# Four graph layers in one kernel: the last rows of the output in long operations, with TensorE adding x and h, and three hand-written orders for layer 3

## The chip, the core and the metric

The kernel runs on one core of a Trainium2 chip. The metric is the device time in microseconds (us) of one execution, given as the median of several runs. The profile is of one execution, and its span (first to last instruction) is a little shorter than the device time.

## What is computed

Four layers work on 3327 nodes with 64 features and one dense 3327 x 3327 matrix `adj`; each adds its result to x. Layers 0 to 2 are a gated graph network of two rounds, a hyperbolic one, and a weighted sum over neighbours. The change lies in layer 3, whose reference is, cut down:

```python
h = jnp.maximum(_layernorm(x, axis=-1), 0.0)
x_tan = _logmap0(h, C)
left, right = x_tan @ att_W[:D] + att_b, x_tan @ att_W[D:]
adj_att = jax.nn.sigmoid(left + right.T) * adj
x_local = _logmap(h[:, None, :], h[None, :, :], C)        # for every pair of nodes
support_t = jnp.einsum('ij,ijd->id', adj_att, x_local)
x = x + _proj(_expmap(h, support_t, C), C)
```

So for every pair of nodes there are a distance function, a sigmoid and a product with `adj`, then sums over the neighbours (a vector of 64 and a few single sums for every node), and at the end a formula for each node that gives two factors, ka and ch, with output = x + ka * (the summed vector) + ch * h.

## The kernel before

Nodes are padded to 26 blocks of 128 and lie in pairs of blocks, 13 columns in two groups: the first (columns 0 to 5) and the second (6 to 12). Layers 0 to 2 stream `adj` from memory and are not touched.

Layer 3 has no scheduler: each engine runs its instructions in the order in which Python emits them. `PHASES` cuts the pairs of columns into 13 phases; the first four need the second group alone. A phase has two halves (b = 0, 1), and its work is cut into steps:

- `distances` (L1199, TensorE) writes scalar products to a PSUM pair, `gelus` (L1209) and `square` (L1219, both ScalarE) make the distance function of them.
- `tanh_d` (L1232) and `tanh_t` (L1255) on ScalarE make the attention for the direct and for the turned (symmetric) pairs; `attention_d`, `attention_t` (L1266, VectorE) multiply it with `adj`, whose tiles come in four slots, in order of use.
- `turned` (L1293, TensorE) transposes the distance function into the other PSUM pair, and `factors_t` (L1303) and `factors_d` (L1284, VectorE) multiply it in.
- `gather_t`, `gather_d` and `singles` (all recorded at L1306, TensorE) add the sums up in PSUM banks.

The order of the steps is written out by hand in `ORDER3`: one list for the start, and one that is run for every phase. In a name such as `gelus.0.1.0` the first number says by how many phases the step is late (0 for the current phase, 1 for the one before, -1 for the next), the others name half and chunk. A `tick` moves the generators of `Weave` on by a step. The one that matters is `nodes3` for the first group: it prepares that group's nodes while phase 0 runs. Its parts are the LayerNorm (L973 to L1002, with the table loads of ScalarE at L992 and L965), xd (L1004), the transposes of xd (L502) and their copies xs (L1024) and xw (L1025, L1026), the attention products (L1033), the packs and rows of bf16 terms (L1073 to L1097, with transposes at L1092), and the attention rows leftb (L1115 to L1120).

The end is `finish_f` for the second group and `finish` for the first: copies of the sums from PSUM (L1376, L1378), their products and squares (L1385, L1387), small sums (L1395), the single sums turned to nodes (copied at L1439, multiplied with `pick` at L1444 into the bank of the small sums, `dots`), and the summed vectors transposed to nodes (L1406), which stay in PSUM as `nat`. About 30 small VectorE operations (L1459 to L1496) make ka and ch. The output then comes block by block: ScalarE multiplies h with ch for 24 blocks (L1504), VectorE does nat * ka + x for each of 26 (L1507), adds the two for three groups of 8 blocks (L1512) and does the last two one by one (L1515), and four stores go out (L1518).

Of the kernel before, what the change touches and what calls it, by code (L numbers as in the profile page):

```python
# [12 lines left out]
AF = mybir.ActivationFunctionType  # L13
# [5 lines left out]
D = 64  # L19
P = 128  # L20
# [63 lines left out]
class Weave:  # L84
# [2 lines left out]
    def __init__(self):  # L87
        self.running = []

    def add(self, gen, after=1, behind=None):  # L90
        self.running.append([gen, after, behind])
        return gen

    def runs(self, *gens):
# [2 lines left out]
    def tick(self):  # L97
        for item in list(self.running):
            if self.runs(item[2]):
                continue  # L100
            item[1] -= 1
            if item[1] <= 0:
                try:
                    item[1] = next(item[0]) or 1
                except StopIteration:
                    self.running.remove(item)

# [82 lines left out]

def order3(text):
    r = []
    for line in text.split("\n"):
        for name, *args in (w.split(".") for w in line.split()):
            r.append((name, *map(int, args)))
    return r
# [4 lines left out]
    order3(t)  # L203
    for t in (
        """
        distances.0.0.0 gelus.0.0.0 distances.0.0.1 tick.0 tanh_t.0.0.0 tanh_t.0.1.0
        attention_t.0.0 tick.0 gelus.0.0.1 distances.0.1.0 square.0.0 tanh_d.0.0 tanh_t.0.0.1
        gelus.0.1.0 attention_d.0.0 tanh_t.0.1.1 distances.0.1.1 tick.1 tick.0 tick.0 gelus.0.1.1
        tick.0 tick.0 square.0.1 turned.0.0.0
        """,  # L210
        """
        factors_t.1.0.0 tick.0 distances.0.0.1 tick.1 turned.1.0.1 tanh_t.0.0.0 attention_d.1.0
        tick.1 singles.2.1 gelus.0.0.1 distances.0.1.0 tick.1 square.0.0 factors_t.1.0.1 tick.0
        turned.1.1.0 gelus.0.1.0 tanh_d.0.0 factors_d.1.0 tick.1 tick.0 tick.0 end.2
        attention_t.1.1 gather_t.1.0.0 tick.0 factors_t.1.1.0 distances.0.1.1 singles.1.0
        gelus.0.1.1 square.0.1 turned.1.1.1 attention_d.1.1 tanh_t.0.0.1 tick.1 distances.-1.0.0
        tanh_t.0.1.0 tick.0 factors_t.1.1.1 tick.0 factors_d.1.1 tanh_d.0.1 tick.0 turned.0.0.0
        attention_t.0.0 tanh_t.0.1.1 gelus.-1.0.0 gather_t.1.0.1 gather_t.1.1.0 gather_d.1.0
        gather_t.1.1.1 gather_d.1.1
        """,  # L220
    )
]


class Stream:
# [67 lines left out]
def gnn_kernel(ctx: ExitStack, tc: tile.TileContext, t, out):  # L293
# [169 lines left out]
    def big(g, name):  # L463

        if g.part is None:
            a = p0.tile([P, GROUPS[1].nb, D], F32, name=name, tag="b_" + name)
        else:

            if name not in bigs:
                bigs[name] = p0.tile([P, GROUPS[1].nb, D], F32, name=name, tag="b_" + name)  # L470
            a = bigs[name][:, 6 * g.part :, :]
        return a[:, : g.nb, :]

    def flat(a):
        return a.rearrange("p a d -> p (a d)")

    def pair(i):

        return ps.tile([P, 1024], F32, name="pair", tag=f"pair{i}")

    def bank(i):
        return ps.tile([P, 512], F32, name="bank", tag=f"bank{i}")
# [678 lines left out]
    def columns(a, n):  # L1161
        return a[:, : 2 * n * P].rearrange("p (k c) -> p k c", k=2)
# [142 lines left out]
    def add(out, lhsT, rhs):  # L1305
        T.matmul(out, lhsT=lhsT, rhs=rhs, start=False, stop=True, skip_group_check=True)  # L1306

    @step3
    def gather_d(m, b):
        a = columns(dirs[m, b], PHASES[m].n)  # L1310
        for c, ts, first in PHASES[m].runs:
            for p, o, lo, hi in runs(ts, place):
                for k in range(2):
                    add(
                        p[k * D : (k + 1) * D, o : o + (hi - lo) * P],
                        xd[:, 2 * c + b, :],
                        a[:, k, (first + lo) * P : (first + hi) * P],
                    )
# [18 lines left out]
    @step3  # L1337
    def singles(m, b):

        nonlocal late_  # L1340
        sums_ = ps_
        if (m, b) == (n_all - 1, 1):

            sums_ = late_ = pair(0)[:, : 2 * P]
            V.memset(late_, 0.0)
        a = columns(dirs[m, b], PHASES[m].n)
        direct, turned_ = [], []
        for c, ts, first in PHASES[m].runs:
            i = 0
            while i < len(ts):  # L1350
                n = min(2 - ts[i] % 2, len(ts) - i)
                o = ts[i] % 2 * P
                for k in range(2):
                    rhs = a[:, k, (first + i) * P : (first + i + n) * P]
                    direct.append(((k, 1 - b, slice(o, o + n * P)), ts[i], 2 * c + b, rhs))
                i += n
        for e, (_, c, j) in enumerate(PHASES[m].turned):
            o = c % 2 * P
            for h_ in range(2):
                rhs = trs[m, b][:, (2 * e + h_) * P : (2 * e + h_ + 1) * P]  # L1360
                turned_.append(((h_, b, slice(o, o + P)), c, 2 * j + b, rhs))
        while direct or turned_:
            for q, most in ((direct, 2), (turned_, 4)):
                for _ in range(min(most, len(q))):
                    single(sums_, *q.pop(0))
# [37 lines left out]
    def by_nodes(g, m, out_, lo, hi):  # L1403

        for c in range(lo, hi):
            T.transpose(  # L1406
                out_[:, (c - lo) * P : (c - lo + 1) * P], m[:, c * P : (c + 1) * P], ident
            )
        for k in range(2 * lo, 2 * hi):
            nat[2 * g.c0 + k] = out_[:, (k - 2 * lo) * D : (k - 2 * lo + 1) * D]  # L1410

    nat, dots = {}, None

    def finish_f():
        nonlocal dots
# [16 lines left out]
    def finish():  # L1432
# [1 line left out]
        parts_ = [(0, 512, x2_), (512, g.w, ps_[:, 2 * P :])]  # L1434
        m = copied(g, parts_)
        ws_ = squares(g, parts_, m)
        pp = flat(big(GROUPS[1], "sq"))[:, : 4 * P].rearrange("p (s i c) -> p s i c", s=2, i=2)
        for s, a in enumerate((ps_, late_)):
            S.activation(pp[:, s], a[:, : 2 * P].rearrange("p (i c) -> p i c", i=2), AF.Copy)  # L1439
        for a, b, _ in parts_:  # L1440
            added(g, ws_, a // P, b // P)
        for i in range(2):
            for s in range(2):
                T.matmul(  # L1444
                    dots[:, 64:96].rearrange("p (r i h) -> p i r h", i=2, h=2)[:, i],
                    lhsT=pp[:, s, i],
                    rhs=pick,
                    start=s == 0,
                    stop=s == 1,
                )  # L1450
        by_nodes(g, m, pair(1), 0, g.n)
        ds, hs, ss = dots[:, 64 : 64 + NB], dots[:, :NB], dots[:, 32 : 32 + NB]


        f = wide3("f", "d2")
# [43 lines left out]
            for b in range(2)  # L1499
        )  # L1500

        steps_ = [(0, 8), (8, 16), (16, 24), (24, NB)]
        for k in range(24):
            S.activation(w2[:, k, :], h[:, k, :], AF.Copy, scale=ch[:, k : k + 1])  # L1504
        for lo, hi in steps_:
            for k in range(lo, hi):
                V.scalar_tensor_tensor(  # L1507
                    w1[:, k, :], nat[k], ka[:, k : k + 1], xn[:, k, :], op0=OP.mult, op1=OP.add
                )
        for lo, hi in steps_:  # L1510
            if hi < NB:
                V.tensor_add(w1[:, lo:hi], w1[:, lo:hi], w2[:, lo:hi])  # L1512
            else:
                for k in range(lo, hi):
                    V.scalar_tensor_tensor(  # L1515
                        w1[:, k, :], h[:, k, :], ch[:, k : k + 1], w1[:, k, :], op0=OP.mult, op1=OP.add
                    )
            nc.sync.dma_start(out[:, lo:hi, :], w1[:, lo:hi])  # L1518

    def bound():  # L1520

# [188 lines left out]


    turn["banks"] = (1,)
    gen_s = weave.add(nodes3(gs_, m_s))

    with ExitStack() as cf:
        wk = cf.enter_context(right("wkf"))

        ps_, x2_, late_ = bank(0), None, None
        V.memset(ps_, 0.0)

        within = n3.tile([1, 1], I32, name="within")
        final = None
        for m, order in [(0, ORDER3[0])] + [(m, ORDER3[1]) for m in range(n_all + 2)]:
            for name, late_by, *args in order:
                if name == "tick":

                    if late_by or m < BETWEEN:  # L1730
                        weave.tick()
                elif have(m - late_by) and (m - late_by, name, *args) not in made3:
                    made3.add((m - late_by, name, *args))
                    for _ in STEPS3[name](m - late_by, *args) or ():
                        pass
            if m == WITHIN + 1:
                ok = nc.values_load(within, min_val=0, max_val=1)
        weave.until(final)
        finish()
# [372 lines left out]
```

## Time and profile before

| | |
|---|---|
| time, median of 3 runs | 701.61 us (699.39 to 702.45) |
| span of the profiled execution | 696.4 us |
| mean granted TensorE clock | 0.966 |
| TensorE (PE) busy | 632.6 us, 91% |
| VectorE (DVE) busy | 460.0 us, 66% |
| ScalarE (ACT) busy | 399.3 us, 57% |
| chain that ended last | PE 73%, DMA 11%, DVE 8%, ACT 5% |
| layer 3, first distances to last instruction | from 423.5 us to 696.4 us |

On a page, the busy tenths show for each of 40 slices how full an engine was, and PEclk the TensorE clock that was granted, in tenths. Where an engine sat idle, the profile names what ended the wait. The chain that ended last is followed back from the last instruction: at each step to what released it. A line of code such as L1306 can be that of a helper that several steps use; then the tiles tell which step it is.

### The profile page before, as it was taken

How to read it: one execution, taken by the hardware profiler on the slowest of the kernel's cores; microseconds unless marked ns; L12 is line 12 of the kernel's file. 1: busy time of each engine (PE TensorE's matmuls, PEld its weight loads, DVE VectorE, ACT ScalarE, POOL GpSimd, SP SyncE). 2: the span in 40 equal slices, each digit the busy share in tenths (PEclk: the TensorE clock that was granted, in tenths of full speed). 3: DMA queues.
4: the chain of work that ended last, by engine and by line, in shares of the span. 5: the costliest groups of instructions: out<-in, count | busy, mean ns of one | idle time of the engine just before them, and what ended most of it. 6: DMA issues, size and time to landing. Idle time of an engine off the chain costs nothing.

```text
span 696.4 us, 13369 instructions
## 1 busy us (share of the span) xinstructions
PE 632.6 (91%) x5648; PEld 358.8 (52%) x5648; DVE 460.0 (66%) x745; ACT 399.3 (57%) x575; POOL 5.9 (1%) x11
## 2 busy tenths in 40 slices
PE   3988999999979999879998996599999999999990
PEld 2433343344324333457875663466666666666770
DVE  4323766444678605786457656489889998888776
ACT  3102200311464203588888788599999898898814
POOL 0000000000000000200000000000000000000000
PEclk9999999999999999999999999599999999999995
DMA  8999998399967999988787863036676666656401
GB/s 342 416 418 416 382 361 299 134 388 416 417 263 279 412 421 416 410 303 292 284 317 261 303 203 135 0 118 201 201 223 210 209 200 201 198 185 198 150 3 53
DMA packets 32611, 185.18 MB, mean 266 GB/s; under 512 B 3616, under 2 KB 4384, under 8 KB 32544
## 3 DMA queue, kind: packets, MB, share of 16 engines
q1 hardware_dynamic: 32544, 184.25, 71.8%
q8 instruction: 46, 0.75, 0.4%
q14 instruction: 21, 0.17, 0.1%
HBM read 183.39 MB, written 0.85 MB: 265 GB/s over the span
## 4 chain that ended last, share of the span: by engine, by line
PE 73%; DMA 11%; DVE 8%; ACT 5%; issue 1%; SPq 0%; ACTq 0%; DVEq 0%
PE bank L627 24%; PE bank L1306 17%; DMA adj<-in_adj 10%; PE pair L1199 8%; PE pair L1293 6%; PE pair L1605 6%; PE bank L1629 5%; PE pair L731 2%; ACT w L1617 1%; DVE mask L1574 1%; PE pair L532 1%; PE bank L1395 1%; DVE w L1507 1%; DMA xn<-in_x 1%; PE bank L1033 1%
## 5 line engine op out<-in xcount | busy, mean ns | idle before, releaser
L627 PE MATMUL bank<-adj,m_a 128*64 128x384 f32 (+1 forms) x832 | 157.3, 524 | 7.5 <-DMA adj<-in_adj 6.7
L627 PEld LDWEIGHTS bank<-adj,m_a 128*64 128x64 f32 x832 | 57.6, 139 | 97.0 <-issue 73.8
L1617 ACT ACTIVATE w<-pair,ebias 128x896 uint16<-128x896 f32 (+1 forms) x101 | 93.8, 953 | 17.0 <-PE pair L1605 15.7
L627 PE MATMUL bank<-adj,m_b 128*64 128x384 f32 (+1 forms) x416 | 76.7, 515 | 0.8 <-ACT hm L716 0.8
L1574 DVE TENSOR_SCALAR mask<-adj 128x1792 bf16<-128x1792 f32 (+1 forms) x52 | 53.8, 1054 | 25.9 <-PE pair L1605 24.1
L1255 ACT ACTIVATE tr<-leftb,righth 128x256 f32<-128x256 f32 x156 | 66.4, 495 | 0.0
L1303 DVE SCALAR_TENSOR_TENSOR tr<-pair,tr 128x1024 f32<-128x1024 f32 (+3 forms) x52 | 50.0, 961 | 23.1 <-PE pair L1293 20.8
L359 DVE SCALAR_TENSOR_TENSOR edges<-adj,edges 128x1792 bf16<-128x1792 f32 (+1 forms) x24 | 44.9, 1890 | 28.6 <-DMA adj<-in_adj 28.5
L1209 ACT ACTIVATE sq<-pair 128x1024 f32<-128x1024 f32 (+1 forms) x52 | 47.4, 912 | 23.9 <-PE pair L1199 22.7
L1629 PE MATMUL bank<-w,m_b 128*64 128x384 bf16 (+1 forms) x416 | 60.6, 341 | 0.0
L1199 PE MATMUL pair<-xs 64*128 64x512 f32 (+3 forms) x120 | 55.6, 549 | 1.2 <-ACT sq L1209 1.2
L1199 PE MATMUL pair<-xs,xw 64*128 64x512 f32 (+3 forms) x120 | 55.6, 549 | 1.1 <-ACT sq L1209 1.1
L716 ACT ACTIVATE hm<-bank 64x384 f32<-64x384 f32 (+1 forms) x8 | 4.1, 512 | 88.2 <-DVE mh L715 88.0
L1293 PE MATMUL pair<-ident,sq 128*128 128x128 f32 x312 | 46.6, 286 | 6.6 <-ACT sq L1219 6.3
L1284 DVE SCALAR_TENSOR_TENSOR dir<-sq,dir 128x1792 f32<-128x1792 f32 (+2 forms) x27 | 52.4, 1945 | 0.0
L1266 DVE SCALAR_TENSOR_TENSOR dir<-dir,adj 128x1792 f32<-128x1792 f32 x26 | 52.4, 2015 | 0.0
L627 PEld LDWEIGHTS bank<-adj,m_b 128*64 128x64 f32 x416 | 29.0, 137 | 44.9 <-issue 42.4
L1293 PEld LDWEIGHTS pair<-ident,sq 128*128 128x128 f32 x312 | 34.1, 143 | 28.9 <-issue 11.9
L1232 ACT ACTIVATE dir<-leftb,righth 128x1792 f32<-128x1792 f32 (+6 forms) x38 | 48.5, 1307 | 0.0
L1219 ACT ACTIVATE sq<-sq,hg 128x1792 f32<-128x1792 f32 x26 | 46.5, 1790 | 0.7
L1266 DVE SCALAR_TENSOR_TENSOR tr<-tr,adj 128x1280 f32<-128x1280 f32 (+2 forms) x26 | 45.5, 1750 | 0.0
L1306 PE MATMUL bank<-dir,xd 128*64 128x384 f32 (+3 forms) x264 | 43.6, 460 | 0.0
(305 smaller groups left out, 983.5 us busy)
## 6 DMA issues: line engine op xcount, KB each, us to landing
adj<-in_adj SPq DMA_DIRECT2D x110, 896.0 KB, 5.8
adj<-in_adj SPq DMA_DIRECT2D x93, 768.0 KB, 8.2
adj<-in_adj SPq DMA_DIRECT2D x12, 640.0 KB, 4.0
out<-w SPq DMA_DIRECT2D x3, 256.0 KB, 3.2
xn<-in_x SPq DMA_DIRECT2D x3, 192.0 KB, 4.8
w_l<-in_w_l SPq DMA_DIRECT2D x1, 460.0 KB, 9.8
xn<-in_x SPq DMA_DIRECT2D x1, 256.0 KB, 6.7
w_all<-in_w_all SPq DMA_DIRECT2D x1, 67.5 KB, 12.7
```

The lines of the kernel that those rows point to most:

```text
L627: T.matmul(acc[q][h * D : (h + 1) * D, : hi - lo], lhsT=m[:, k, :], rhs=a[:, h * g.w + lo : h * g.w + hi], start=first, stop=last,)
L1199: T.matmul(p[:, o : o + n], lhsT=l, rhs=r, start=not rows, stop=rows)
L1232: S.activation(columns(dirs[m, b], ph.n)[:, :, first * P : first * P + n], left_of(ph.g)[:, :, o : o + n], AF.Tanh, bias=righth[:, 2 * c + ...
L1255: S.activation(a[:, e * 2 * P : (e + 1) * 2 * P].rearrange("p (b c) -> p b c", b=2), left_of(ph.s)[:, :, o : o + P], AF.Tanh, bias=righth[ ...
L1266: V.scalar_tensor_tensor(a[:, :w], a[:, :w], 1.0, stream.tile(stream.now), op0=OP.add, op1=OP.mult)
L1284: V.scalar_tensor_tensor(a[:, :, cs], s[:, :, cs], HD, a[:, :, cs], op0=OP.add, op1=OP.mult)
L1293: T.transpose(p[:, o : o + P], columns(sqs[m, b], PHASES[m].n)[:, k, i * P : (i + 1) * P], ident,)
L1303: V.scalar_tensor_tensor(a, pts.pop((m, k, "t"))[:, :n], HD, a, op0=OP.add, op1=OP.mult)
L1306: T.matmul(out, lhsT=lhsT, rhs=rhs, start=False, stop=True, skip_group_check=True)
L1574: V.tensor_scalar(masks[n][:, :w], a, 0.0, None, op0=OP.not_equal)
L1617: S.activation(w, e, AF.Relu, bias=ebias)
L1629: T.matmul(acc2[i][q][h * D : (h + 1) * D, : hi - lo], lhsT=p[:, 2 * c + a, :], rhs=ws[n][:, h * g.w + lo : h * g.w + hi].bitcast(BF16), s ...
```

## The change

It has four parts.

1. Output rows in long operations. For the blocks 12 to 25, TensorE writes x to two PSUM banks (an fp32 product with the identity) and adds ScalarE's products of h and ch. VectorE multiplies nat with ka for many blocks at once, ka being broadcast along the features, and then adds the bank. Blocks 6 to 11 are done by VectorE alone and are stored first; blocks 0 to 5 have x added by VectorE, and h by way of ScalarE. The aim is fewer and longer operations on VectorE, and output that is stored as it becomes ready.
2. The single sums of one half go to the node form earlier, before the last `gather_d`, and both halves have their result in a PSUM bank of their own (`ds_`) instead of in `dots`.
3. `ORDER3` has three lists: one for the start, one for the phases in between, one for the last phase. In the first, `turned.0.0.0` stands behind the first `distances` of the next phase, and `gelus.0.1.1` behind more ticks.
4. `WAITS3` says after how many ticks each step of the first group's `nodes3` is made.

```diff
-    def add(self, gen, after=1, behind=None):
-        self.running.append([gen, after, behind])
+    def add(self, gen, after=1, behind=None, waits=()):
+        self.running.append([gen, after, behind, list(waits)])
...
                     item[1] = next(item[0]) or 1
+                    if item[3]:
+                        item[1] = item[3].pop(0)
...
-        distances.0.0.0 gelus.0.0.0 distances.0.0.1 tick.0 tanh_t.0.0.0 tanh_t.0.1.0
-        attention_t.0.0 tick.0 gelus.0.0.1 distances.0.1.0 square.0.0 tanh_d.0.0 tanh_t.0.0.1
-        gelus.0.1.0 attention_d.0.0 tanh_t.0.1.1 distances.0.1.1 tick.1 tick.0 tick.0 gelus.0.1.1
-        tick.0 tick.0 square.0.1 turned.0.0.0
+        distances.0.0.0 gelus.0.0.0 distances.0.0.1 tanh_t.0.1.0 tick.0 tanh_t.0.1.1 tick.0 tick.0
+        tick.1 gelus.0.0.1 square.0.0 distances.0.1.0 gelus.0.1.0 tick.0 distances.0.1.1 tick.0
+        tick.0 tick.0 gelus.0.1.1 tick.0 tick.0 square.0.1 tick.1 tick.0 tick.1 tick.1 tick.0
+        tick.1 tick.1 distances.-1.0.0 turned.0.0.0 tick.0 tick.0 tanh_d.0.1 tick.0 gelus.-1.0.0
...
     @step3
     def gather_d(m, b):
+        nonlocal pp_
+        if (m, b) == (n_all - 1, 1):
+            assert (m, "singles", 0) in made3
+            pp_ = flat(big(GROUPS[1], "sq"))[:, : 4 * P].rearrange("p (s i c) -> p s i c", s=2, i=2)
+            copied_singles(0, ps_)
...
-            sums_ = late_ = pair(0)[:, : 2 * P]
+            ends_ = pair(0)
+            sums_ = late_ = ends_[:, : 2 * P]
             V.memset(late_, 0.0)
+            ds_ = ends_[:, 512:544]
+            picked(0)
...
-        for k in range(24):
+        for lo, hi, a in sums_x:
+            T.matmul(a, lhsT=ident, rhs=flat(xn[:, lo:hi]), start=True, stop=False)
+        for k in [*range(12, NB), *range(6)]:
             S.activation(w2[:, k, :], h[:, k, :], AF.Copy, scale=ch[:, k : k + 1])
-        for lo, hi in steps_:
-            for k in range(lo, hi):
-                V.scalar_tensor_tensor(
-                    w1[:, k, :], nat[k], ka[:, k : k + 1], xn[:, k, :], op0=OP.mult, op1=OP.add
-                )
...
+        for lo, hi, a in sums_x:
+            T.matmul(a, lhsT=ident, rhs=flat(w2[:, lo:hi]), start=False, stop=True)
...
+        times(6, 12, a[:, 6 * D :])
+        plus(6, 12, xn[:, 6:12])
+        V.tensor_mul(w2[:, 6:12], h[:, 6:12], bc(ch[:, 6:12]))
+        plus(6, 12, w2[:, 6:12])
+        store(6, 12)
+        for lo, hi, b in larger[::-1]:
+            times(lo, hi, b)
+        times(0, 6, a[:, : 6 * D])
+        plus(0, 6, xn[:, 0:6])
+        for lo, hi, b in sums_x:
+            plus(lo, hi, b.rearrange("p (k d) -> p k d", d=D))
+            store(lo, hi)
+        plus(0, 6, w2[:, 0:6])
+        store(0, 6)
...
-    gen_s = weave.add(nodes3(gs_, m_s))
+    gen_s = weave.add(nodes3(gs_, m_s), waits=WAITS3)
...
-        for m, order in [(0, ORDER3[0])] + [(m, ORDER3[1]) for m in range(n_all + 2)]:
+        begin, loop, rest = ORDER3
+        orders = [(0, begin)] + [(m, loop) for m in range(1, n_all - 1)] + [(n_all - 1, rest)]
+        for m, order in orders:
```

The loop list differs from the one before in a few places, among them `tanh_d.0.1`, which stands ahead of `tanh_t.0.1.0`, and `gather_t.1.1.1`, which stands ahead of `gather_t.1.1.0`. The last list takes the steps of the last two phases together and puts `turned.1.1.0` ahead of more ticks, and so ahead of the small sums of `finish_f`.

## The prediction

> **What bounds the kernel now.** I read the page first: the busy slices and the granted TensorE clock of the whole span, to see where TensorE is not the limit.
>
> ```profile
> PE   3988999999979999879998996599999999999990
> ACT  3102200311464203588888788599999898898814
> PEclk9999999999999999999999999599999999999995
> ```
>
> TensorE is near full almost everywhere. Two places matter to this change: a dip two thirds of the way through, and the last slices, empty and at the low clock. Next the busy time by stretches of 10 us, which puts times to them (columns: busy us of PE, PEld, DVE, ACT, POOL, each with a count; then granted clock, DMA share, GB/s).
>
> ```profile
> 430.00:440.00 10.00, 2.60 (x15) 1.41 (x12) 7.52 (x19) 8.63 (x12) 0.00 (x0) 0.73 0.00 1
> 440.00:450.00 10.00, 6.67 (x27) 4.93 (x27) 2.42 (x10) 3.80 (x6) 0.00 (x0) 0.50 0.00 0
> 450.00:460.00 10.00, 9.71 (x82) 6.34 (x80) 8.27 (x26) 7.94 (x10) 0.00 (x0) 0.75 0.02 4
> 600.00:610.00 10.00, 10.00 (x120) 6.50 (x113) 9.51 (x6) 9.97 (x17) 0.00 (x0) 1.00 0.68 225
> 660.00:670.00 10.00, 10.00 (x148) 7.47 (x146) 9.90 (x8) 0.84 (x2) 0.00 (x0) 1.00 0.01 2
> 680.00:697.00 17.00, 0.00 (x0) 0.00 (x0) 10.27 (x53) 7.56 (x27) 0.00 (x0) 0.51 0.16 54
> ```
>
> So layer 3 has three parts. From 432.9 to 448.4 TensorE mostly waits for the node preparation of the first half (the interlude). From about 451 to 679.4 it never rests, and its own work is the limit. From 679.4 on it does nothing, and VectorE sets the end (the tail). The timeline of the interlude shows who holds whom (start us, length us, engine, line, tile, then idle before and releaser):
>
> ```profile
> 432.63 0.81 ACT L1209 ACTIVATE sq<-pair 128x768 f32<-128x768 f32 x1
> 433.33 0.83 ACT L988 ACTIVATE xc<-h_n 128x768 f32<-128x768 f32 x1
> 434.19 1.28 ACT L992 ACT_TABLE_LOAD   x1
> 439.13 1.76 PE L1293 MATMUL pair<-ident,sq 128*128 128x128 f32 x7 [6.29 <-ACT sq L1219]
> 440.68 1.06 PE L502 MATMUL bank<-ident,xd 128*128 128x128 f32 x4
> 441.78 0.69 DVE L1024 COPY xs<-bank 128x512 f32<-128x512 f32 x1 [2.12 <-PE bank L502]
> 445.76 2.72 PE L1033 MATMUL bank<-w_all,xs 128*128 128x4 f32 x12 [1.32 <-ACT xw L1026]
> 448.41 1.22 PE L1199 MATMUL pair<-xs 64*128 64x512 f32 x1
> ```
>
> The chain is LayerNorm on ScalarE and VectorE, xd (ready at 437.92 + 0.96 = 438.88), the transposes of xd (L502), three copies, the attention products (L1033), and only then the distances of phase 1 (L1199). L502 was queued behind the eight transposes of turned(0,0,0) (L1293), which waited for a square on ScalarE until 439.13. The timeline of the tail:
>
> ```profile
> 683.57 5.83 ACT L1504 ACTIVATE w<-h,f 128x64 f32<-128x64 f32 x24 [0.60 <-DVE f L1495]
> 683.74 2.39 DVE L1507 SCALAR_TENSOR_TENSOR w<-pair,f,xn 128x64 f32<-128x64 f32 x12
> 686.05 2.77 DVE L1507 SCALAR_TENSOR_TENSOR w<-bank,f,xn 128x64 f32<-128x64 f32 x14
> 688.73 1.89 DVE L1512 TENSOR_TENSOR w<-w 128x512 f32<-128x512 f32 x3
> 689.44 2.45 SPq L1518 DMA_DIRECT2D out<-w  x4
> ```
>
> VectorE works without a gap from 683.74 to 690.9; the last of the four stores starts to issue at 691.4 and lands 3.0 us later.
>
> [...] clock 0.50 from 434.55 until 455.0[...], and 0.50 again from 680.4. [...] the trace has 683 ns (L1512). [...] ScalarE's xw waits for VectorE's xs, 4.7 us in 2 times, with the two reading one bank.
>
> **Part by part.** *Beginning list and WAITS3 (interlude).* On ScalarE the gelu of distances(0,1,1), 0.81 us, moves from ahead of the square of hr (L988) to behind the two table loads; one tanh piece (0.50) moves ahead, into time when ScalarE waited. The square L988 then follows L981 directly, about 432.4 instead of 433.33, and the loads, the roots, h and xd all come 0.9 earlier: xd at 438.0. On TensorE turned(0,0,0) moves behind L502, L1033 and the first distances of phase 1. L502 starts at 438.1, not 440.47 (its weight load). The rest of the chain keeps its lengths, so L1033 starts at 443.4 and the distances at 446.0: 2.4 earlier than 448.41. Given back: the eight transposes now lie where TensorE has no idle time. At full clock they take 1.02 (eight in the chain of waits), at half about 2.0 (seven in 1.76). I take 1.02[...]. They also fill a gap before L1092 (450.92 to 451.21, about 0.2 with the clock). Behind factors_t(0,0,0) on VectorE, which waits for these transposes until about 450.2, stand four small pack copies and the copy of rows_i; it ran at 451.24 before, so nobody is later. Sum: -2.4 - 0.2 + 1.0 = -1.6. Bounds: -0.6 with transposes at half clock[...].
>
> *Loop list.* The order of forms on TensorE in phases 2 to 10 is unchanged, and so is VectorE's; on ScalarE a tanh_d goes ahead of a tanh_t, both between the same square and gelu. TensorE is 10.00 of 10 busy here and its work stays: 0.
>
> *Last list (drain).* The same TensorE work again, reordered. In 640 to 673 its only wait is about 0.3 us, at 656.1 to 656.43, for factors_t on VectorE. Moving turned(1,1,0) ahead of finish_f's small sums takes that wait away: -0.3. VectorE is full from 656.3 to 672.6, so no more can come.
>
> *Single sums in another bank.* Half of L1444, four matmuls of about 0.12, moves from the tail into the drain. The ScalarE copy ahead of it is free, as ScalarE is idle for 12.2 us before m_t. But TensorE is full on both sides of the move, so the sum to 679.4 is the same: 0.
>
> *Output rows (tail).* Removed: 26 + 2 operations at 0.19 spacing and 3 at 0.60, 7.2 us on VectorE. Added: two operations on 512 columns at 0.60 and nine on 384 at [...] 0.47, or 5.4 us. Two fp32 products with x run at 679.5 beside VectorE's small operations: nothing. The two products with h wait for ScalarE (0.239 a row): 8 rows are ready at 685.6, 14 at 687.0. TensorE was idle for 4 us, so I take the half clock, as with the 512-column product at 448.41 (1.02 + 0.85 = 1.87 us for its two parts). First product done at 687.6, second (1.4) at 689.1. VectorE would reach the first sum at 683.74 + 4 x 0.47 + 0.60 + 3 x 0.47 = 687.6: no wait. It reaches the second at 688.3 and waits until 689.1; behind it stand only the last sum and store. VectorE ends at 690.1 instead of 690.9. One store has gone at 685.6 and the others don't queue up, so the last issues at 690.15, not 691.4: -1.25. At full clock it would be -2.0; with a slower landing (192 KB rather than 64 KB; 256 KB took 3.2 against 3.0) and a store in the queue, -0.8.
>
> Total: -1.6 - 0.3 - 1.25 = -3.2, so 701.6 - 3.2 = 698.4.
>
> **Rivals.** *A, the clock helps.* In the interlude TensorE is now busy without a gap from 443.4, [...] and the products in the tail meet a full clock: -2.8 - 0.4 - 2.0 = -5.2, 696.4. For it: in 448.2 to 451.6 one small gap stood, and the clock did not return. Against: 4 us idle ahead of the products. *B, the interlude gives nothing.* The moved transposes at half clock (2.0), or a later rows_i or rows_j copy that holds phase 1, eat the 2.4; only the tail is left: about -1.2, 700.4. For it: VectorE and ScalarE are 8.3 and 7.9 of 10 busy in 450 to 460. *C, slower.* ScalarE is 9.97 of 10 busy at 600 to 610. If the new tanh order made one gelu late in each of 9 phases by 0.4, TensorE would wait 3.6 that it does not now; with B that is +2.4, 704.0. Against: ScalarE waits for TensorE's distances there, 22.7 us in 32 times over the layer, so it has slack.
>
> **How the numbers follow.** Forecast 0.5, A 0.2, B 0.2, C 0.1. The line of 0.5% lies at 698.1, just under the forecast. A and nearly half of the forecast lie below it: faster 0.44; the rest of it and B: same 0.46; slower 0.1. Runs of the kernel before lie 3 us apart, so some 1.2 is added to the bounds -5.2 and -1.2: 695.9 to 701.0, which leaves out C and a tail of the others.
>
> **What would show it.** Right: L502 on xd follows the xd product at once, L1033 starts about 2.4 us earlier relative to the last LayerNorm reduce of that half, the stretch from phase 2 to the last phase keeps its length within 0.5 us, and VectorE works about 6.4 us from the first output row to the last. Wrong: waits of TensorE on ScalarE's gelu in the loop, a wait of factors_t(0,0,0) that delays phase 1, or output products that end after 690.

## The result, and the profile after

| | before | after |
|---|---|---|
| time, median of 6 runs each | 699.65 us (698.27 to 702.45) | 694.99 us (693.88 to 696.10) |
| ratio, 95% interval | | 0.9926 (0.9903 to 0.9948) |
| span of the profiled execution | 696.4 us | 692.6 us |
| mean granted TensorE clock | 0.966 | 0.973 |

The changed kernel is faster by 0.5 to 1.0%. The forecast was 698.4 us and its range ended at 695.9; the measured time lies 0.9 us below the range. Two more comparisons, below, gave ratios of 0.9967 and 0.9940. Weighted by their intervals the three make 0.9945 (0.9933 to 0.9957), or -3.8 us (-4.7 to -3.0); they lie further apart than their own intervals would lead one to expect, so this last interval is too narrow. There are two questions: where the time came from, and why a forecast of -3.2 us missed the absolute time.

The page of the changed kernel, busy tenths of 40 slices and the granted clock:

```profile
PE   2988999999979999889998997599999999999994
ACT  3102200311364303588888888699999988888813
PEclk9999999999999999999999999699999999999996
```

The dip is still there, one tenth shallower in PE and in the clock. In the last slice TensorE now has work, four tenths of it. The stretches of 10 us, columns as before:

```profile
430.00:440.00 10.00, 2.46 (x14) 1.12 (x10) 7.99 (x20) 8.85 (x12) 0.00 (x0) 0.82 0.01 2
440.00:450.00 10.00, 7.62 (x28) 5.15 (x28) 2.84 (x15) 5.35 (x10) 0.00 (x0) 0.50 0.00 0
450.00:460.00 10.00, 9.64 (x121) 6.61 (x122) 9.73 (x14) 9.41 (x11) 0.00 (x0) 1.00 0.21 67
600.00:610.00 10.00, 10.00 (x116) 6.49 (x116) 8.51 (x6) 9.64 (x18) 0.00 (x0) 1.00 0.66 184
660.00:670.00 10.00, 10.00 (x149) 7.87 (x143) 9.55 (x10) 0.39 (x1) 0.00 (x0) 1.00 0.01 2
680.00:692.00 12.00, 3.36 (x4) 1.13 (x4) 6.77 (x18) 5.10 (x21) 0.00 (x0) 0.59 0.22 78
```

The clock was at half from 436.4 to 450.1, four windows of 3.41 us (in the traces before and after, all changes of the clock lie on one grid of 3.41 us, and the spells at half clock in the interlude given below, 3.4 to 23.9 us, are one to seven steps of it; a step is called a window), and in 450 to 460 it is full throughout (0.75 before). TensorE is as full as before in the loop (600 to 610) and the drain (660 to 670). The timeline of the interlude (start us, length us, engine, line, tile, then idle before and releaser):

```profile
432.33 0.84 ACT L1008 ACTIVATE xc<-h_n 128x768 f32<-128x768 f32 x1
437.94 1.12 PE L522 MATMUL bank<-ident,xd 128*128 128x128 f32 x4 [5.49 <-DVE xd L1024]
443.07 2.72 PE L1053 MATMUL bank<-w_all,xs 128*128 128x4 f32 x12 [1.32 <-ACT xw L1046]
445.73 1.22 PE L1219 MATMUL pair<-xs 64*128 64x512 f32 x1
448.16 1.97 PE L1313 MATMUL pair<-ident,sq 128*128 128x128 f32 x8
450.06 0.38 PE L1219 MATMUL pair<-xs 64*128 64x128 f32 x1
```

The square of hr (L1008) stands 1.0 earlier than before. L522 starts 0.06 us after xd is written (436.92 + 0.96) and no longer behind the eight transposes. L1053 and the first distances of phase 1 (445.73) follow 2.69 and 2.68 earlier, of which 0.13 is only that layer 3 starts earlier in this trace (423.39 against 423.52). The transposes (L1313) now come behind those distances, at the half clock, and the next distances stand at 450.06. The tail:

```profile
681.09 4.88 ACT L1539 ACTIVATE w<-h,f 128x64 f32<-128x64 f32 x20 [0.60 <-DVE f L1528]
683.16 3.36 PE L1541 MATMUL bank<-w,ident 128*128 128x512 f32 x4 [3.42 <-ACT w L1539]
683.49 4.45 SPq L1550 DMA_DIRECT2D out<-w  x4
685.50 0.68 DVE L1547 TENSOR_TENSOR w<-w,bank 128x512 f32<-128x512 f32 x1
686.55 0.55 DVE L1547 TENSOR_TENSOR w<-w,bank 128x384 f32<-128x384 f32 x1 [0.37 <-PE bank L1541]
687.02 0.55 DVE L1547 TENSOR_TENSOR w<-w 128x384 f32<-128x384 f32 x1
```

From its first output row at 681.25 to its end at 687.57 VectorE takes 6.32 us, against 7.27. It waits once, 0.37 us, for the second of TensorE's two products with h (L1541).

### The profile page after: what moved, and what is told of

The parts are those of the page before. It is cut to its first block, busy times and chain, and to the rows that moved or that the text cites. A ratio compares the mean times of both kernels' runs of the same rounds, so it can differ in the third digit from the quotient of the medians.

```text
span 692.6 us, 13360 instructions
## 1 busy us (share of the span) xinstructions
PE 636.2 (92%) x5656; PEld 360.0 (52%) x5656; DVE 458.7 (66%) x725; ACT 399.2 (58%) x571; POOL 5.9 (1%) x11
## 4 chain that ended last, share of the span: by engine, by line
PE 72%; DMA 13%; DVE 8%; ACT 5%; issue 1%; SPq 1%; DVEq 0%; ACTq 0%
PE bank L647 21%; PE bank L1326 17%; DMA adj<-in_adj 12%; PE pair L1219 8%; PE pair L1653 6%; PE pair L1313 6%; PE bank L1677 5%; PE pair L751 2%; ACT w L1665 1%; DVE mask L1622 1%; PE pair L552 1%; DMA xn<-in_x 1%; PE bank L1423 1%; PE bank L522 1%; PE bank L1053 1%
## 5 line engine op out<-in xcount | busy, mean ns | idle before, releaser
L1229 ACT ACTIVATE sq<-pair 128x1024 f32<-128x1024 f32 (+1 forms) x52 | 47.5, 913 | 20.8 <-PE pair L1219 20.0
L1313 PE MATMUL pair<-ident,sq 128*128 128x128 f32 x312 | 46.1, 285 | 0.1
L1313 PEld LDWEIGHTS pair<-ident,sq 128*128 128x128 f32 x312 | 34.0, 143 | 22.2 <-issue 11.8
```

What stands on the lines that cost most here:

```text
L1313: T.transpose(p[:, o : o + P], columns(sqs[m, b], PHASES[m].n)[:, k, i * P : (i + 1) * P], ident,)
```

## Experiments

One measure of a trace is used below: the stretch from the first distances of layer 3 to VectorE's first output row, and from there to the end of the span. It leaves out layers 0 to 2, which nothing here touches; behind them the first distances of layer 3 stand anywhere from 421.8 to 425.7 us in the traces. The times scatter: in the session with most runs, 67 runs of the unchanged kernel before lie between 695.4 and 703.5 us, and the longer ones tend to have the lower mean clock (correlation -0.77). Each trace is of one run, which can lie off the median of its kernel: 2.5 us under it in e4, 2.7 in e14, and in e8, the fastest of 14, 3.6.

### The parts alone

Each of these is the kernel before with a piece of the change.

```diff
# e1_rows: as in the diff's lines on sums_x, times, plus and store, nothing else
+        sums_x = [(12, 20, bank(0)), (20, NB, bank(1)[:, : 6 * D])]
# e2_singles: copied_singles, picked and ds_ alone
+            ds_ = ends_[:, 512:544]
+            picked(0)
# e3_begin: the first list and WAITS3; the old list from phase 1 on
+        orders = [(0, begin)] + [(m, loop) for m in range(1, n_all + 2)]
# e4_loop_last (and e14): the old first list and phase 0, then the new lists
+        orders = [(0, begin), (0, second)] + [(m, loop) for m in range(1, n_all - 1)] + [(n_all - 1, rest)]
# e13_all_lists: all three new lists and WAITS3, old singles and output rows
+        orders = [(0, begin)] + [(m, loop) for m in range(1, n_all - 1)] + [(n_all - 1, rest)]
# e6_begin_rows: e3 and e1 together
```

> The kernel before with one part of the change: the rows of the output in long operations, the sums of x and of the products with h for 14 of the 26 columns on TensorE. Theory (the forecast's tail step): VectorE needs about 6.3 us instead of 7.2 from the first row of the output to the last, and the last store lands a little sooner; the time falls by 1.25 us, to a ratio of 0.998, within 0.8 to 2.0 us. Rival (TensorE's products at the half clock hold VectorE up): 0 to -0.4 us. In the trace VectorE should wait less than 0.5 us in all for the products.

> The kernel before with one part of the change: the single sums of one half copied and summed earlier, into another bank. Theory: two copies and two products of 2 columns move from after the last transposes' wait into an earlier gap; the path goes by the other half's copy, so 0 us, within 0.3. Rival (those copies stood on the path): -0.5 us.

> The kernel before with one part of the change: the order of the first list and the counts of waits of the second group's LayerNorm; all later lists as before. Theory (the order, and with it an earlier return of TensorE's full clock): -2.4 us, ratio 0.9966, and the full clock back within 7 us of the start of the twelve 4-column products, which stand about 2.7 us earlier after the first distances. The forecast's own size: -1.6 us. Rival (the interlude is given back in the loop): 0. In the trace the distances of the second phase's start should stand 2.4 us earlier after the first distances.

> The kernel before with one part of the change: the order of the lists from the second phase on and of the last phase; the first list as before. Theory: the loop moves by less than 0.1 us and the last list by 0 to -0.3 us, so 0 to -0.3 in all, no difference that can be measured. Rival (in the loop TensorE waits for the gelu that now stands behind a tanh): +0.5 us or more.

> The changed kernel without the new lists from the second phase on and without the early single sums: new first list with its waits, and output rows. Theory (the parts add up, and the loss of the later lists alone came from their standing behind the old first list): -1.4 - 0.8 = -2.2 us, ratio 0.9969, and 0.5 to 1.5 us slower than the changed kernel. Rival (the later lists are a loss in the changed kernel too): faster than the changed kernel by 1 us or more.

> The kernel before with all three lists and the counts of waits, without the output rows and the early single sums. Theory (the later lists lose only behind the old first list, where TensorE stood 0.73 us for a bank; behind the new one they cost nothing): the same as with the first list alone, -1.4 us, and up to 0.3 less time; ratio 0.997 to 0.998. Rival (the later lists are a loss everywhere): 0 to +0.3 us against the kernel before.

> The later lists behind the old first list once more, on another chip perhaps. If the loss of 1.7 us is the kernel's, it stands again at 0.6 us or more, of which the trace shows at most 0.5 (the wait of 0.73 us for the bank); if it was an accident of that hour, the ratio is within 0.0008 of 1. In the profile the second 384-column product with one row group waits for VectorE's leftb again.

> The changed kernel itself, timed in more runs beside the parts. If the forecast's sum is right and the first comparison of few runs lay low, the difference is about -3.2 us (ratio 0.9954), and the parts' sum agrees with it once the lists from the second phase on are no loss beside the new first list. If something that the forecast left out works, the difference stays at -4.7 us (ratio 0.9933) or more. In the profile the stretch from the first distances of the last stage to the first of its second phase is again 22.3 us (before: 24.9).

> The changed kernel once more, since its two comparisons gave -4.7 and -2.4 us. The sum of its parts in the traces (the stretch to the first output row 1.8 us shorter, from there to the end 1.35) says -3.15, ratio 0.9955; a value between -2 and -4.2 would bear that out.

Measured (the us are the ratio's distance from 1 times the median of before in that session; the two last columns are from the traces):

| kernel | ratio, 95% interval | us | to the first row | first row to end |
|---|---|---|---|---|
| before | 1 | 0 | 260.22 | 12.7 |
| e1 rows | 0.9989 (0.9977 to 1.0002) | -0.8 | 259.39 | 11.3 |
| e2 singles | 1.0002 (0.9984 to 1.0019) | +0.1 | 260.43 | 12.9 |
| e3 first list | 0.9980 (0.9967 to 0.9993) | -1.4 | 258.53 | 12.6 |
| e4 later lists | 1.0024 (1.0008 to 1.0039) | +1.7 | 260.74 | 12.8 |
| e14 the same again | 1.0003 (0.9984 to 1.0022) | +0.2 | 260.46 | 12.9 |
| e13 all lists | 0.9973 (0.9959 to 0.9986) | -1.9 | 258.04 | 12.6 |
| e6 first list and rows | 0.9964 (0.9950 to 0.9979) | -2.5 | 259.67 | 11.3 |
| after | 0.9926 (0.9903 to 0.9948) | -5.2 | 257.86 | 11.3 |
| e5 after | 0.9967 (0.9947 to 0.9987) | -2.3 | 258.20 | 11.3 |
| e15 after | 0.9940 (0.9920 to 0.9959) | -4.2 | 259.14 | 11.3 |

(The -5.2 of the first comparison is by its ratio; the medians lie 4.7 apart.)

What follows. The five traces with the old first list (before, e1, e2, e4, e14) need 260.25 us to the first row on average, the three of the changed kernel 258.40: -1.85. Without e4 and e14, whose later lists add a wait (below), it is 260.01 and -1.6. From there to the end, the old output rows take 12.6 to 12.9 us and the new ones 11.3 in each trace: -1.4 on average. Together -3.0 to -3.3. The single sums are worth nothing that can be measured, as forecast. In the traces the output rows are worth what the forecast said; by time e1 has only -0.8, with an interval from -1.6 to +0.1. For e3 the earlier chain came as expected and the time is nearer to -1.6 than to -2.4; the clock was back 8.4 us behind the start of the twelve 4-column products, and not within 7.

The later lists are the unclear piece. Alone they came out 1.7 us slower in one session and 0.2 in the next (weighted by the intervals, 1.1, from 0.3 to 1.9), while the trace of e4 shows one wait that before doesn't have:

```profile
464.77 0.32 PE L1138 MATMUL bank<-rows_i,onesl 12*128 12x384 bf16 x1 [0.73 <-DVE leftb L1143]
```

Two products of the attention rows (12 rows each) go to one PSUM bank, and TensorE stands 0.73 us ahead of the second until VectorE has copied the first (L1143). e14 has it too (0.86 us). In the changed kernel's timeline of that stretch no such wait stands, and e13, with the new first list ahead, is no slower than e3. So the later lists are no loss behind the new first list and have this wait behind the old one. The two traced runs are faster than their medians, so whether the 1.7 of the first session is more than the wait of 0.7 and scatter stays open.

### The two moves of the interlude

The forecast put 0.9 us on the gelu's move behind the table loads, and 1.5 on the eight transposes' move behind L502. e10 makes only the second, in the kernel before. e9 puts the transposes of the changed kernel back into idle time, but behind the first four transposes of xd.

```diff
# e10_turned_later, to the kernel before
-        tick.0 tick.0 square.0.1 turned.0.0.0
+        tick.0 tick.0 square.0.1
# e9_turned_in_gap, to the changed kernel
-        tick.0 tick.0 gelus.0.1.1 tick.0 tick.0 square.0.1 tick.1 tick.0 tick.1 tick.1 tick.0
-        tick.1 tick.1 distances.-1.0.0 turned.0.0.0 tick.0 tick.0 tanh_d.0.1 tick.0 gelus.-1.0.0
+        tick.0 tick.0 gelus.0.1.1 tick.0 tick.0 square.0.1 turned.0.0.0 tick.1 tick.0 tick.1 tick.1 tick.0
+        tick.1 tick.1 distances.-1.0.0 tick.0 tick.0 tanh_d.0.1 tick.0 gelus.-1.0.0
```

> The kernel before with one move of the change: the eight transposes of the first phase behind the first distances of the second, nothing else (the gelu stays ahead of the LayerNorm's squares). Theory: the transposes of xd follow xd at once, so the stretch from the first distances of the stage to those of the second phase shrinks from 24.9 to 23.1 or 23.2 us, and 1.0 us of it is given back behind them: -0.7 us, ratio 0.999. The remaining 0.9 or so of the changed kernel's 22.3 is then the gelu's place. Rival (the gelu's move is what counts, and the transposes hid behind it): the stretch stays above 24 us.

> The changed kernel with one move undone in part: the eight transposes of the first phase stand between the four and the two transposes of xd, where TensorE waits for ScalarE's copies, and no longer behind the first distances of the second phase. Theory (the forecast's +1.0: there they lie in the path of a busy TensorE, here in idle time): the distances of the second phase start as early as in the changed kernel (22.3 us after the first distances of the stage), and the whole is 1.0 us shorter, 0.7 to 1.3 in a comparison of profiles once the clock's return is taken out. Rival (they hold up the two transposes of xd): the stretch grows by 0.5 us or more, and nothing is gained.

The timeline of e10: xd was written from 438.88 on (0.96 us), and L502 follows it.

```profile
439.89 1.12 PE L502 MATMUL bank<-ident,xd 128*128 128x128 f32 x4 [6.35 <-DVE xd L1004]
447.68 1.22 PE L1199 MATMUL pair<-xs 64*128 64x512 f32 x1
```

From the first distances of the layer (424.48) to these it took 23.20 us. With the whole old first list and no filling it was 24.89 or 24.90 in all five traces; in e3, e5, e13 and the first trace of the changed kernel it was 22.34 or 22.35. So the transposes' move is worth 1.69 us on this chain and the gelu's place the other 0.86, against 1.5 and 0.9 forecast. By time e10 is -1.1 us (ratio 0.9984, 0.9971 to 0.9996). (In e6 and e15 the stretch was 23.5: there the clock had dropped already at 427, and distances of phase 0 that take 0.69 us at the full clock took 1.22.)

The timeline of e9:

```profile
437.93 1.92 PE L1313 MATMUL pair<-ident,sq 128*128 128x128 f32 x8
440.15 0.69 PE L522 MATMUL bank<-ident,xd 128*128 128x128 f32 x2 [0.30 <-ACT xw L1046]
448.43 0.58 PE L1219 MATMUL pair<-xs 64*128 64x128 f32 x1 [1.11 <-ACT sq L1229]
```

The eight transposes take 1.92 us between the two groups of L522 and hold nothing up: the stretch is 22.35. What they leave behind the distances is not free, though. There TensorE now waits 1.11 us for ScalarE's gelu (L1229; it writes the tile `sq`), which reads the PSUM pair that the next distances write. So the next distances start 3.62 us after the first ones (444.81); in the changed kernel 4.33 (450.06 - 445.73). The transposes cost 0.7 there, not 1.0, and not their 1.97 us at the half clock: they lie for the most part in a wait that the forecast had not seen. e9's time is 694.42 us, ratio 0.9927 (0.9900 to 0.9955), which overlaps that of the changed kernel; its trace, with the clock back only at 452.6, shows no gain in the whole stretch (258.54). The gain of 1.0 us that was expected does not show.

### The clock

In all thirteen traces above the clock dropped to half in the interlude, where TensorE idles, and stayed there for 13.7 to 20.5 us (23.9 in e6). Four kernels put useless products there, x with the identity, whose results nobody reads (e12's last ones are overwritten by those that count).

```diff
+    def warm(n, i):
+        p = pair(i)
+        for _ in range(n):
+            T.matmul(p[:, :512], lhsT=ident, rhs=flat(xn[:, 0:8]), start=True, stop=True)
# e7_filled_after, e12_gap_filled (6 for 5; no 2, its place has the transposes)
+        if g is gs_:
+            warm(5, 1)
         for p, i0, i1 in transposed(g, xd[:, sl, :]):
+            if g is gs_:
+                warm(2 if i0 == 0 else 1, 1)
# e8_filled_before, e11_filled_before_7 (7 for 5): the first ones ahead of turned(0, 0, 0)
# e12_gap_filled: e9's list, and at the end, ahead of the products of x
+        for _ in range(3):
+            T.matmul(bank0_, lhsT=ident, rhs=flat(xn[:, 12:20]), start=True, stop=True)
```

> The changed kernel with eight products of x (128x512 f32 with the identity, their results read by nobody) put into TensorE's idle time in the interlude: five ahead of the transposes of xd, two and one behind them. Theory (the granted clock, dropped for want of work in the idle time, sets how long the chain after it takes): no drop at 434 to 436, the four and two transposes take about 0.56 and 0.35 us instead of 1.12 and 0.69, the twelve 4-column products about 1.4 instead of 2.72, and the some 5 us of half clock after them are saved by half: -3 to -4.7 us against the changed kernel. Rival (VectorE and ScalarE set the chain, or the products delay what follows): 0 or slower.

> The kernel before with the same eight products in its interlude (results read by nobody), so that the clock does not drop there. Theory: -3.5 to -5 us against the kernel before. What is then left between this kernel and the changed kernel so filled is the order alone, without the clock: the chain 1.6 to 2.5 us earlier less 1.0 for the eight transposes, and 0.8 to 1.25 at the end, so 1.5 to 2.8 us. Rival (the change's gain in the interlude is only an earlier return of the clock): the two filled kernels differ by the output rows alone, 0.8 to 1.25 us.

> The kernel before, its interlude filled with ten products of x (results read by nobody), seven of them ahead of the eight transposes, so that TensorE has no idle stretch there that is long enough to lose the clock. Theory (the earlier filled kernel lost it for 3.4 us at 438.8, because its five products ended 2 us too soon): no drop, -3.5 to -5 us against the kernel before, ratio 0.993 to 0.995. Rival (filling is worth nothing in this order): within 1 us of the kernel before.

> The changed kernel with the eight transposes between the two groups of transposes of xd, six products of x ahead of these and one behind (results read by nobody), and three more products of x at the end of the kernel, ahead of those that are used (overwritten by them), to hold the clock for the last products. Theory: the first filled kernel's -7.6 us, 1.0 less for the transposes and 0.3 to 0.4 for the last products, so about -9 us against the kernel before, ratio 0.987. Rival (the end's products come at the half clock and hold up the last ones): no better than the first filled kernel.

| kernel | median us | ratio, 95% interval | to the first row | clock at half in the interlude |
|---|---|---|---|---|
| e7 after, filled | 690.55 | 0.9887 (0.9867 to 0.9906) | 254.08 | never |
| e12 after, gap used and filled | 692.10 | 0.9895 (0.9867 to 0.9924) | 253.96 | never |
| e8 before, filled with 8 | 697.66 | 0.9992 (0.9976 to 1.0008) | 257.29 | 438.8 to 442.3 |
| e11 before, filled with 10 | 697.01 | 0.9965 (0.9949 to 0.9981) | 260.39 | 426.7 to 430.2 (phase 0), 447.2 to 454.1 |

The timeline of e7:

```profile
432.76 4.56 PE L991 MATMUL pair<-xn,ident 128*128 128x512 f32 x10
438.32 0.66 PE L522 MATMUL bank<-ident,xd 128*128 128x128 f32 x4 [1.00 <-DVE xd L1030]
442.74 1.50 PE L1063 MATMUL bank<-w_all,xs 128*128 128x4 f32 x12 [0.45 <-ACT xw L1056]
444.17 0.69 PE L1229 MATMUL pair<-xs 64*128 64x512 f32 x1
445.44 1.09 PE L1323 MATMUL pair<-ident,sq 128*128 128x128 f32 x8
446.63 0.37 PE L1229 MATMUL pair<-xs 64*128 64x128 f32 x1
```

With the clock held, L522 takes 0.66 instead of 1.12 us, the twelve 4-column products 1.50 instead of 2.72, the first distances 0.69 instead of 1.22. They stand 20.41 us after the layer's first distances instead of 22.34, and the first output row 254.1 instead of 258.4 on average. That is 4.3 us in the trace, 5.2 between the medians of one session, and the forecast of this run was 3 to 4.7. All five runs (689.5 to 691.9) lie under all 23 of the changed kernel (693.6 to 698.0).

In e12 the same line of the second distances shows why using the gap earns nothing more:

```profile
448.58 0.37 PE L1229 MATMUL pair<-xs 64*128 64x128 f32 x1 [1.11 <-ACT sq L1239]
```

They start 2.45 us after the first ones, as in e7 (446.63 - 444.17 = 2.46): at the full clock the eight transposes (1.09) fit into the 1.11 us for which TensorE otherwise waits for ScalarE's gelu. With the products at the end VectorE's part is 6.05 us against 6.17 in e7, but from the first row to the end it is 11.4 against 11.2. So e12 is no better than e7 and misses its -9, as its rival said; the rival's reason was not seen, since the added products ran at the full clock, which dropped only at 682.6.

In the old order the filling gained less: 0.6 us by the median in e8 and 2.4 in e11, where -3.5 to -5 was forecast for both; e11 is also more than its rival allowed (within 1 us). The two filled kernels e7 and e8 lie 7.1 us apart, further than either side of e8's expectation said. Why is only in part shown. In the trace of e8 the five products ended 2 us before the transposes could start, and the clock dropped at 438.8 for one window. That run still took only 694.05 us, as much less as forecast; the other 13 took 695.5 to 700.0, and no trace shows what they lost. In e11 the clock dropped at 447.2, in a wait behind the first distances of phase 1 that the new order does not have:

```profile
448.23 1.04 PE L1100 MATMUL bank<-identb,pack 128*128 128x128 bf16 x8 [1.45 <-DVE pack L1085]
```

But the wait had lasted only 0.44 us then (so how long an idle stretch must be for that is not shown), and e8's trace has the same one, inside another window, without a drop:

```profile
448.54 0.62 PE L1100 MATMUL bank<-identb,pack 128*128 128x128 bf16 x8 [1.45 <-DVE pack L1085]
```

In e11 the window that ended at 447.2 also held the twelve 4-column products (1.4 us), in e8 the window around the wait almost none of them. So the two traces differ in where the windows fall; that this decided, and that the new order is what lets the clock be held, is not shown.

## Why the prediction missed, point by point

**The base: the step that failed.** "Total: ... so 701.6 - 3.2 = 698.4". The 701.61 was a median of three runs. With three more, the kernel before measured 699.65, and in the four sessions of the experiments 698.67, 698.18, 698.86 and 699.53, over 173 runs. The base was thus 2.0 to 3.4 us high, about as much as the change itself. The trace from which all parts were costed was of a run of 698.2 us, so the parts of a faster run were taken from the median of slower ones. Of the 3.4 us between 698.4 and 694.99 the base makes 2.0. The other 1.5 are the difference of the first comparison, 4.7 where 3.2 was forecast; over the three comparisons it is 3.8, and 3.2 lies in that interval. From 699.65 the forecast would have been 696.5, and 694.99 within a range as wide as the one given. The range was too narrow for such a base: "some 1.2 is added to the bounds", but 695.9 is only 0.5 under A's 696.4, and 701.0 only 0.6 above B's 700.4.

**Begin list and WAITS3: -1.6 forecast.** The chain was forecast 2.4 earlier and is 2.55 (24.89 to 22.34), of it 1.69 and 0.86 for the two moves by e10. The +1.0 for the transposes was mis-sized: e9 shows 0.7 at the half clock, e12 nothing at the full one, because of the wait for ScalarE's gelu. So the mechanism stood, and -2.55 + 0.7 is -1.85; the gap ahead of L1092, 0.29 us in the kernel before, is gone as forecast and can add to it. e3 measured -1.4 (-2.3 to -0.5) for the whole step.

**The clock.** The forecast took the moved transposes at the full clock, which was my estimate, and put an earlier return of the clock into rival A; the size of that, -2.8, was an estimate too. Both orders vary from trace to trace: from the first distances of phase 1 to the clock's return it took 6.6, 3.5, 6.6, 6.7 and 3.4 us in the five traces with the old first list, and 5.7, 4.4, 5.7, 5.0, 5.7 and 5.2 with the new (e3, after, e5, e6, e13, e15). On average that is 5.4 and 5.3: the clock comes back as much earlier as the chain does, and no more. The first trace after has the shortest of the new ones beside one of the long ones before; that makes this pair of traces 3.8 us apart instead of some 3.2, by the scatter of the clock's return and not by a step of the change.

**Loop list: 0.** Right inside the change: e13 is within the interval of e3. Behind the old first list TensorE has a wait of 0.7 to 0.9 us for a bank, for which no step of mine looked: the lists were costed one by one, each beside its own predecessor.

**Last list: -0.3.** The gain came, and was lost again. TensorE's lead over the kernel before grew from 2.51 us at the last phase's distances (645.32 against 647.83) to 2.95 at the last two transposes (665.53 against 668.48), so 0.44. The wait that was to go is 0.18 us in the trace (L1293 at 656.43), not 0.3, so it makes less than half of that; where the rest comes from is not shown. e13 shows as much against e3, from the loop and the last list together and with the clock back equally late in both: 258.04 against 258.53 to the first row. But at VectorE's first small operation of the end the lead was 2.48 (676.30 against 678.78). The products of the moved single sums (L1445) took 0.5 us ahead of L1423, as forecast; behind it the four that were left should have given that back, but the clock had dropped at 675.4, and they held the transposes up for 0.76 us, against 0.45 in e12, where it had not (last section).

**Single sums: 0.** Right (e2: +0.1, -1.1 to +1.3).

**Output rows: -1.25.** Right in the traces, -1.4 on average. That VectorE took 6.32 us, where about 6.4 was forecast, is luck in part, as two errors cancel: its operations took 5.95 us (5.4 forecast; the last two, on 384 columns, start 0.47 us apart, as taken, and last 0.55 each), and it waited 0.37 for the second product (0.8 forecast). The products with h ran at the half clock, as taken (0.50 from 682.2 on), in 3.36 us (1.87 + 1.4 forecast).

**Rivals.** A's -5.2 is what the ratio of the first comparison shows, but by luck: the products in the tail met the half clock, and the clock came back no sooner behind the chain than before. C's wait on gelus in the loop does not occur; TensorE is 10.00 of 10 busy there. B falls with e3 and e10.

## What to carry to other kernels

Before a change of half a per cent is forecast in absolute time, count the runs of the base: three runs of a kernel that scatters by 1% place it no better than the change. Where an engine waits ahead of a chain, look in the trace for the next wait behind the chain as well; work moved there may be free, as the transposes of 1.09 us were in e12, in a wait of 1.11. And where TensorE idles ahead of a latency chain, a few useless dense products can be worth more than the order itself: 8 of them gave 4 to 5 us in the new order. In the old one 8 and 10 gave 0.6 and 2.4, with runs that were up to 8 us apart, so one trace does not tell whether the clock is held.

## What the hardware showed unexpectedly

In the changed kernel TensorE lost the full clock at 675.4, at the end of a window in which the profile shows it as full. The end of the drain, first the timeline, then busy time in stretches (columns as before):

```profile
672.57 1.05 PE L1423 MATMUL bank<-halves,h_n 128*128 128x2 f32 x8
675.27 0.92 PE L1445 MATMUL pair<-pick,sq 128*128 128x16 f32 x4
676.03 1.52 PE L1434 MATMUL pair<-ident,m_t 128*128 128x128 f32 x6
```

```profile
672.00:675.30 3.30, 3.30 (x39) 2.89 (x29) 0.06 (x1) 0.38 (x1) 0.00 (x0) 1.00 0.00 0
675.40:678.70 3.30, 3.30 (x13) 2.62 (x13) 2.07 (x18) 0.69 (x2) 0.00 (x0) 0.50 0.01 2
```

PE is 3.30 of 3.30 us busy ahead of the drop at 675.4, with products of 2 columns (L1423) for most of it. The four 16-column products behind it then take 0.92 us instead of 0.60 (e12, whose clock held there), and the six transposes 1.52 instead of 0.85.

The other traces bear this out. In twelve of the seventeen, 2.3 to 2.8 us of one window go to these 2-column products, and the clock dropped at the end of that window each time, although PE is busy in all of it. In the other five (before, e2, e4, e9, e12) they fall across two windows, at most 1.9 us in one. There the clock held at the end of the first window, and in e9 and e12, where TensorE had other work, at the end of the second as well.

The 12 products of 4 columns (L1053) show the same for the clock's return. In seven traces of the changed order (after, e3, e5, e6, e9, e13, e15) PE is busy through a whole window at the half clock, with 1.1 to 2.5 us of it in these products, and none of these windows brought the full clock. In the changed kernel that is the window that ended at 446.7. In the traces before and after, seven windows at the half clock were full of other products (the one from 675.4 among them), and each brought it, as the next one did here (450.1).

So in these traces no window with 2.3 us or more in products of 2 columns kept the full clock, and none of the seven at the half clock with 1.1 us or more in products of 4 columns brought it back, though PE was busy throughout. The ends of products are modelled in the profile, so how much of the array's time the narrow ones fill is not shown, nor that this is the cause. Nor was the window ahead of a drop always idle: the one that ended at 434.5 in the kernel before had 1.34 us of work. And the spell in the interlude varied from run to run, 4 to 7 windows for nearly the same work. Of the same code up to there, e1 with the clock back 3.5 us after the distances of phase 1 and the kernel before with 6.6 differ by 0.8 us to the first row (259.39 and 260.22).
